# Merging a head's softmax parts on 32 partitions in layer 2's cross attention

## The chip, the core and the metric

The kernel runs on one core of a Trainium2 chip. A core has five engines with a queue each: TensorE (PE in the profile, its weight loads PEld), VectorE (DVE), ScalarE (ACT), GpSimd (POOL) and SyncE (SP, which issues most DMAs). They work side by side and wait for each other by semaphores. The metric is the device time of one execution in microseconds (us), the median of several runs.

## What is computed

Four layers of cross attention and feed-forward on an input x of 4 x 256 x 256, all in float32. The change lies in the cross attention of layer 2:

```python
q = rope(rms_norm((x @ wq).reshape(B, L, 16, 128)))     # B = 4, L = 256
k_full = [rms_norm(ctx @ wk_ctx), rope(rms_norm(x @ wk))]   # 1601 + 256 keys, 4 heads of keys
v_full = [ctx @ wv_ctx, x @ wv]
scores = jnp.einsum('bhlm,...', q, k_full) * scale + mask   # own keys causal
probs = jax.nn.softmax(scores, axis=-1)
out = jnp.einsum('bhlm,bmhd->blhd', probs, v_full)
return out.reshape(B, L, 16 * 128) @ wo
```

That is shortened: rope is applied to q and to the own keys, not to the keys of the context, and each key head serves four query heads. A softmax over one query's keys needs their maximum and the sum of their exponentials.

## The kernel before

The stage `l2_xattn` works through 16 units: batch 0 to 3 by key head 0 to 3, and in a unit through four query heads h, 64 heads in all. A unit's keys `kT` and values `va` have 15 tiles of 128 keys.

A head's 256 queries are cut into 8 blocks of 32, two blocks to each of four steps c. In `scores` (lines 1451 to 1475) the products of one block with all keys are spread over the partitions: partition 32a + j holds query j of the block against the keys 32a to 32a+31 of each tile. So each query lies on four partitions, one in each group of 32. Every partition finds the negated maximum of its own part (`nm`, line 1467, VectorE) after the mask is added (line 1464), and ScalarE computes the exponentials `p` with it and sums them up (`sm`, line 1471). There are two pairs of score banks (`ps_s`, `bufs=2`): the product for step c waits until the exponentials of step c-2 have been read from theirs.

The four parts of a query then have to be merged. `merge` (1477 to 1501) does it for a whole head: TensorE transposes `nm` and `sm` (each 128 partitions x 8 blocks) to 8 partitions x 128 in PSUM (`tm`, lines 1482 and 1483); VectorE takes the least negated maximum of the four parts (`lo`, 1487) and the differences (1489), ScalarE the exponentials of these (`em`, 1490); VectorE multiplies them with the sums (1492), adds the four parts (1494), takes the reciprocal (1495) and multiplies (1496). That gives each part's share, still as 8 x 128. TensorE transposes it back (1498), and VectorE copies it to `rm`, 128 x 8 (1500).

GpSimd then scales the eight `p` blocks with these shares (`scale`, line 1507), VectorE transposes them in squares of 32 x 32 (`turn`, 1513), and TensorE multiplies with the values into `o` (`values`, lines 1517 to 1526; 30 instructions), which ScalarE copies to `at`. Every four heads `project` multiplies with `wo` and adds to x.

The heads are overlapped by generators: while the scores of head h are issued, `softmax_steps` of head h-1 and `value_steps` of head h-2 are advanced, and between them `prep` prepares queries, own keys and loads for the next unit. A step of a generator ends at `yield`. In the main loop, `softmax_steps` is advanced once after the scores of c = 0 and 1 (the first part of `merge`, up to its `yield`), a second time at the end of this half, after values, preparation and projection (the rest of `merge` and the scalings), and a third time after the scores of c = 2 and 3 (the turns). The source order sets priorities; each engine's final order is made by a list scheduler when the program is built, except where `keep_in_program_order` pins an instruction. So in the profile `lo` stands between a mask and its maximum.

[...] 4 for scores, 2 for preparation (`ps`), 1 for `tm` (`ps_m`) and 1 for `o` (`ps_o`).

Of the kernel before, what the change touches and what calls it, by code (L numbers as in the profile page):

```python
# [11 lines left out]
F32 = mybir.dt.float32  # L12
# [5 lines left out]
AF = mybir.ActivationFunctionType  # L18
ALU = mybir.AluOpType
AX = mybir.AxisListType  # L20
PSUM = bass.MemoryType.PSUM
DRAM = bass.MemoryType.DRAM

P = 128
# [34 lines left out]
class Kernel:  # L59
# [1185 lines left out]
    def l2_xattn(self):  # L1245
# [8 lines left out]
        nc, tc, i = self.nc, self.tc, self.i  # L1254
        NK, CT = NK2, CT2
        OWN = [(13, 32, P), (14, 160, 96)]
        with ExitStack() as es:
# [1 line left out]
            two = es.enter_context(tc.tile_pool(name="a2", bufs=2, reuse_waits="tile"))  # L1259
            ps_s = es.enter_context(tc.tile_pool(name="a2s", bufs=2, space=PSUM))  # L1260
            ps = es.enter_context(tc.tile_pool(name="a2p", bufs=2, space=PSUM))
            ps_m = es.enter_context(tc.tile_pool(name="a2m", bufs=1, space=PSUM))
            ps_o = es.enter_context(tc.tile_pool(name="a2o", bufs=1, space=PSUM))
            self.take = lambda: ps_s.tile([P, 2, 512], F32, name="fill2", tag="s2")[:, 0, :]

            mask = one.tile([P, 8, 3, 32], F32, name="mask2")
# [41 lines left out]
            def load(g, early):  # L1308
                w = {}
                for n, shape in (("wq", [P, 2, 512]), ("wkc", [P, 2, 256]), ("wks", [P, 2, 256])):  # L1310
                    if n == "wkc" and early:
                        continue
                    w[n] = one.tile(shape, F32, name=n)
                    nc.sync.dma_start(w[n], i["l2_" + n][g])
                return w
# [131 lines left out]
            def tiles_of(c):  # L1447

                return 14 if c < 2 else 15

            def scores(kT, qT, h, c, nm, sm):

                nt = tiles_of(c)
                s = ps_s.tile([P, 2, 512], F32, name="s2")
                for n in range(2):
                    q0 = (2 * c + n) * 32
                    for a in range(4):
                        self.mm(
                            s[32 * a : 32 * a + 32, n, : nt * 32].rearrange("p (t i) -> p t i", i=32),
                            qT[:, h, q0 : q0 + 32], kT[:, :nt, 32 * a : 32 * a + 32], True, True,  # L1460
                        )
                w = (nt - CT) * 32
                sv = s[:, :, CT * 32 : nt * 32]
                nc.vector.tensor_tensor(  # L1464
                    sv, sv, mask[:, 2 * c : 2 * c + 2, : nt - CT, :].rearrange("p n t i -> p n (t i)"), ALU.add
                )
                nc.vector.tensor_reduce(nm[:, 2 * c : 2 * c + 2], s[:, :, : nt * 32], AX.X, ALU.max, negate=True)  # L1467
                p = main.tile([P, 2, NK * 32], F32, name="p2", bufs=8)
                for n in range(2):
                    e = 2 * c + n  # L1470
                    nc.scalar.activation(  # L1471
                        p[:, n, : nt * 32], s[:, n, : nt * 32], AF.Exp, bias=nm[:, e : e + 1],
                        accum_out=sm[:, e : e + 1],
                    )
                return p

            def merge(nm, sm):


                t = ps_m.tile([P, 512], F32, name="tm2")  # L1480
                ct, st = t[:8, 0:P], t[:8, P : 2 * P]
                tc.keep_in_program_order(nc.tensor.transpose(ct, nm, self.ident))
                tc.keep_in_program_order(nc.tensor.transpose(st, sm, self.ident))
                by = lambda ap: ap.rearrange("n (a j) -> n j a", a=4)
                wide = lambda ap: ap[:, :, None].to_broadcast([8, 32, 4])
                lo = self.small.tile([8, 32], F32, name="lo2")
                nc.vector.tensor_reduce(lo, by(ct), AX.X, ALU.min)
                e = self.small.tile([8, P], F32, name="em2", bufs=2)
                nc.vector.tensor_tensor(by(e), wide(lo), by(ct), ALU.subtract)
                nc.scalar.activation(e, e, AF.Exp)  # L1490
                w = self.small.tile([8, P], F32, name="wm2", bufs=2)
                nc.vector.tensor_tensor(w, e, st, ALU.mult)
                tot = self.small.tile([8, 32], F32, name="tot2")
                nc.vector.tensor_reduce(tot, by(w), AX.X, ALU.add)
                nc.vector.reciprocal(tot, tot)
                nc.vector.tensor_tensor(by(e), by(e), wide(tot), ALU.mult)
                yield
                nc.tensor.transpose(t[:, 256:264], e, self.ident[:8, :8])
                r = self.small.tile([P, 8], F32, name="rm2")
                nc.vector.tensor_copy(r, t[:, 256:264])  # L1500
                return r

            def scale(p, r, c):
                nt = tiles_of(c)
                for n in range(2):
                    e = 2 * c + n
                    nc.gpsimd.tensor_scalar(  # L1507
                        p[:, n, : nt * 32], p[:, n, : nt * 32], r[:, e : e + 1], 1.0, ALU.mult, ALU.mult
                    )

            def turn(p, pT, c):
                nt = tiles_of(c)
                nc.vector.transpose(  # L1513
                    pT[:, 2 * c : 2 * c + 2, :nt, :].rearrange("p n t i -> p n (t i)"), p[:, :, : nt * 32]
                )
# [23 lines left out]
            def softmax_steps(hd):  # L1539


                shares = merge(hd["nm"], hd["sm"])
                next(shares)
                yield
                r = yield from shares
                hd["pT"] = main.tile([P, 8, NK, 32], F32, name="pT2")
                for c in range(4):
                    scale(hd["p"][c], r, c)
                yield
                for c in range(4):  # L1550
                    turn(hd["p"][c], hd["pT"], c)
                yield
# [9 lines left out]
            w = load(0, True)  # L1562
            wo = load_out(0)
# [13 lines left out]
            for n, (b, g) in enumerate(units):  # L1577
                kT, va, qT = ready
                last = hd
                ready, pieces = [], None  # L1580
                wo_now = wo
                at = main.tile([P, 4, S], F32, name="at2", bufs=2)
                for h in range(4):
                    hd = {"nm": self.small.tile([P, 8], F32, name="nm2"), "sm": self.small.tile([P, 8], F32, name="sm2"),
                          "p": [], "va": va, "at": at, "h": h, "b": b, "wo": wo_now}
                    for c in (0, 2):
                        step = 2 * h + c // 2
                        for cc in (c, c + 1):
                            hd["p"].append(scores(kT, qT, h, cc, hd["nm"], hd["sm"]))
                        if soft is not None:  # L1590
                            next(soft[0])
                        if pieces is not None and not early:
                            for _ in range(BETWEEN[step]):
                                next(pieces, None)
                        if vals is not None:
                            next(vals)
                        if step == 0 and n + 1 < len(units):
                            b1, g1 = units[n + 1]
                            early = n + 1 < EARLY
                            if not early and (b1 != b or ctx is None):  # L1600
                                ctx = self.load_ctxT(one, b1, 1)
                            w = load(g1, early)
                            pieces = prep(n + 1, w, ctx, ready)
                            if g1 == 0:
                                next(pieces)
                        if step == 4 and n + 1 < len(units):
                            wo = load_out(g1)
                        if pieces is not None:
                            for _ in range((WHEN_EARLY if early else WHEN)[step]):
                                next(pieces, None)  # L1610
                        if step == 5 and last is not None:
                            project(last)
                        if soft is not None and c == 0:
                            next(soft[0])
                    vals = value_steps(soft[1]) if soft is not None else None
                    soft = (softmax_steps(hd), hd)
                if pieces is not None:
                    for _ in pieces:
                        pass
# [595 lines left out]
```

## Time and profile before

| what | us |
|---|---|
| median of 3 runs | 2638.49 (2635.17 to 2639.96) |
| profiled execution, its own time | 2638.45 |
| its span, first to last instruction | 2636.7 |
| layer 2's attention loop, by the trace | about 695 to 1805 |
| TensorE busy over the span | 2491.9 (95%) |
| VectorE | 1480.0 (56%) |
| ScalarE | 1310.9 (50%) |
| GpSimd | 750.8 (28%) |

A few of the groups that the change touches, with the mean duration of one instruction in the stage (64 of each, one for a head): the two transposes into `tm` 273 ns each by the record, the one back 221; `lo` 275, the differences 355, the exponential 293, the product 275, the sum over parts 377, the reciprocal 338, the shares 364, the copy to `rm` 161. Around them, for one head: 8 exponentials of 645 ns on ScalarE, 8 scalings of 657 on GpSimd, 4 turns of 1127 and 4 maxima of 1104 on VectorE.

A row of the profile names the source line, the engine, the operation, the tile written and the tiles read, shapes, count, busy time and mean, and behind the bar the time the engine stood idle before these instructions with what ended most of it. Matmuls overlap in the array, so the durations of their records are longer than their part of the stream; the part is the distance from one start to the next.

### The profile page before, as it was taken

Reading aid. Unit: us, or ns where it says so; the run is one execution under the profiler, and the core shown is the slowest. Engines: PE = TensorE matmul, PEld = TensorE weight load, DVE = VectorE, ACT = ScalarE, POOL = GpSimd, SP = SyncE. Lnnn points to the kernel's source line nnn. Section 1 sums busy time; section 2 is a strip of 40 time slices with the busy share of each in tenths; the row PEclk is TensorE's granted clock in tenths of the full one; section 3 lists DMA queues with packets and bytes.
Section 4 is the critical chain, followed back from the end, with each engine's and each line's share of the span. In section 5 each row is a group of like instructions: output and inputs, shape, how many; then the busy total and the mean of one; then the engine's idle time right before and its main releaser. Section 6 shows DMA issues by size and latency. Waiting matters only on the chain. (4 is left out here: it accounts for less than half of the span.)

```text
span 2636.7 us, 47077 instructions
## 1 busy us (share of the span) xinstructions
PE 2491.9 (95%) x17816; PEld 1517.6 (58%) x17816; DVE 1480.0 (56%) x3039; ACT 1310.9 (50%) x2957; POOL 750.8 (28%) x1030
## 2 busy tenths in 40 slices
PE   7989988898799999999999999998998999999997
PEld 4668967676455555555555555655564544545553
DVE  6344637644587777777777777673334414333323
ACT  2334545433644445444544454442326766757775
POOL 1015646123334343334443434431102001011000
PEclk8989999999999999999999999998999999999998
DMA  5154787615511111111111110004211100000000
GB/s 201 60 199 128 186 174 216 205 56 174 162 38 46 39 37 46 46 38 47 46 46 46 46 46 21 9 1 159 87 66 63 34 2 27 4 3 2 6 6 5
DMA packets 94655, 186.25 MB, mean 71 GB/s; under 512 B 15052, under 2 KB 62864, under 8 KB 93232
## 3 DMA queue, kind: packets, MB, share of 16 engines
q1 hardware_dynamic: 78118, 141.36, 15.8%
q0 software_dynamic: 10416, 28.46, 5.0%
q10 hardware_dynamic: 5898, 13.41, 1.5%
q8 instruction: 145, 2.38, 0.4%
q14 instruction: 78, 0.64, 0.1%
HBM read 136.77 MB, written 46.42 MB: 69 GB/s over the span
## 5 line engine op out<-in xcount | busy, mean ns | idle before, releaser
L1471 ACT ACTIVATE p<-s,nm 128x448 f32<-128x448 f32 (+1 forms) x512 | 326.9, 645 | 423.9 <-DVE nm L1467 259.1
L1932 ACT ACTIVATE e<-s 128x1024 f32<-128x1024 f32 (+1 forms) x448 | 404.2, 960 | 160.8 <-PE s L75 156.1
L75 PE MATMUL s<-kT,qT 128*32 128x448 f32 (+1 forms) x4096 | 470.2, 556 | 10.0 <-ACT p L1471 5.0
L75 PE MATMUL o<-pT,va 128*128 128x256 f32 (+2 forms) x1920 | 432.5, 377 | 6.1 <-DVE pT L1513 6.1
L1507 POOL TENSOR_SCALAR p<-p,rm 128x448 f32<-128x448 f32 (+1 forms) x512 | 323.7, 657 | 369.6 <-DVE rm L1500 339.4
L75 PEld LDWEIGHTS o<-pT,va 128*128 128x128 f32 (+1 forms) x1920 | 345.4, 191 | 93.6 <-issue 51.5
L1513 DVE STREAM_TRANSPOSE pT<-p 128x896 f32<-128x896 f32 (+1 forms) x256 | 283.8, 1127 | 37.1 <-POOL p L1507 33.4
L1467 DVE TENSOR_REDUCE nm<-s 128x2 f32<-128x896 f32 (+1 forms) x256 | 282.6, 1104 | 3.4
L75 PE MATMUL s<-qb,kT 32*128 32x256 f32 (+1 forms) x3328 | 267.7, 405 | 11.0 <-ACT e L1932 11.0
L75 PEld LDWEIGHTS s<-kT,qT 128*32 128x32 f32 x4096 | 123.6, 109 | 265.0 <-issue 222.5
L75 PE MATMUL o<-e,va 128*32 128x256 f32 (+1 forms) x3328 | 236.6, 392 | 1.2 <-DVE os L2029 1.2
L75 PEld LDWEIGHTS s<-qb,kT 32*128 32x128 f32 (+1 forms) x3328 | 163.1, 181 | 105.5 <-issue 75.8
L75 PE MATMUL fill<-wkc_early,ctxT 128*128 128x256 f32 x780 | 189.6, 401 | 11.8 <-ACT kT_early L1227 9.6
L75 PEld LDWEIGHTS fill<-wkc_early,ctxT 128*128 128x128 f32 x780 | 152.1, 199 | 43.1 <-ACT kT_early L1227 15.0
L75 PEld LDWEIGHTS o<-e,va 128*32 128x32 f32 (+1 forms) x3328 | 90.8, 110 | 115.5 <-issue 75.5
L1959 POOL TENSOR_TENSOR x<-x,t 128x32 f32<-128x32 f32 x64 | 14.7, 252 | 439.7 <-DVE t L1954 439.7
L1464 DVE TENSOR_TENSOR s<-s,mask 128x128 f32<-128x128 f32 (+1 forms) x256 | 83.1, 325 | 67.1 <-PE s L75 62.3
L410 POOL DMA_INDIRECT f0xr<-f0xd,f0src x95 | 92.3, 972 | 51.3 <-PE f0tph L467 43.2
L1359 POOL TENSOR_TENSOR qo<-qo,qt 128x512 f32<-128x512 f32 x32 | 40.7, 1273 | 230.6 <-DVE rm L1500 139.4
L1471 ACT ACTIVATION_READ_ACCUMULATOR p<-s,nm 128x1 f32 x512 | 101.7, 199 | 0.0
L1200 ACT COPY kr_early<-fill 128x256 f32<-128x256 f32 (+1 forms) x105 | 37.3, 355 | 97.9 <-PE fill L75 97.7
L75 PE MATMUL f2gu<-f2wgu,f2xsT 128*128 x176 | 84.3, 603 | 0.6 <-ACT f2xsT L72 0.3
(510 smaller groups left out, 3503.7 us busy)
## 6 DMA issues: line engine op xcount, KB each, us to landing
ctxT<-in_ctxT SPq DMA_DIRECT2D x10, 1664.0 KB
f0yd<-f0ys SPq DMA_DIRECT2D x95, 128.0 KB
vd<-va_early SPq DMA_DIRECT2D x90, 128.0 KB
kd<-kT_early SPq DMA_DIRECT2D x45, 256.0 KB
kT<-kd SPq DMA_DIRECT2D x15, 768.0 KB
va<-vd SPq DMA_DIRECT2D x15, 768.0 KB
wq<-in_l_wq SPq DMA_DIRECT2D x16, 512.0 KB
wo<-in_l_wo SPq DMA_DIRECT2D x16, 512.0 KB
```

What stands on the lines that cost most here:

```text
L75: self.nc.tensor.matmul(out, lhsT, rhs, start=start, stop=stop, **kw)
L410: nc.gpsimd.indirect_dma_start(out=t, out_offset=None, in_=xd[:, :], in_offset=bass.IndirectOffsetOnAxis(ap=src[:, n : n + 1], axis=0),)
L1200: nc.scalar.copy(kr[:rows, m : m + n, :], tp[:rows, :n, :HD2])
L1359: nc.gpsimd.tensor_tensor(o1, o1, t2, ALU.add)
L1464: nc.vector.tensor_tensor(sv, sv, mask[:, 2 * c : 2 * c + 2, : nt - CT, :].rearrange("p n t i -> p n (t i)"), ALU.add)
L1467: nc.vector.tensor_reduce(nm[:, 2 * c : 2 * c + 2], s[:, :, : nt * 32], AX.X, ALU.max, negate=True)
L1471: nc.scalar.activation(p[:, n, : nt * 32], s[:, n, : nt * 32], AF.Exp, bias=nm[:, e : e + 1], accum_out=sm[:, e : e + 1],)
L1507: nc.gpsimd.tensor_scalar(p[:, n, : nt * 32], p[:, n, : nt * 32], r[:, e : e + 1], 1.0, ALU.mult, ALU.mult)
L1513: nc.vector.transpose(pT[:, 2 * c : 2 * c + 2, :nt, :].rearrange("p n t i -> p n (t i)"), p[:, :, : nt * 32])
L1932: nc.scalar.activation(e[:kr, :, :n, :], s[t][:kr, :, :n, :], AF.Exp, scale=1.0 / math.sqrt(HD3))
L1959: nc.gpsimd.tensor_tensor(xt, xt, t[:, q], ALU.add)
```

## The change

The two small tiles `nm` and `sm` become one tile `ms` of 128 x 2 x 8. `merge` no longer uses TensorE: VectorE copies the four groups of 32 partitions side by side onto partitions 0 to 31 (`c`, 32 x 4 x 2 x 8, four copies of 32 x 16), so that a query's four parts lie on one partition. Minimum, difference, exponential, product, sum and reciprocal then run on 32 partitions with 32 elements or 8, and the shares are written back with four multiplications of 32 x 8, one to each group of partitions of `rm`. The `yield` moves: it stood in front of the transpose back, and stands now behind the exponential, so that product, sum, reciprocal and shares belong to the second step. The PSUM bank of `tm` goes to `o`, which has two banks now.

```diff
-            ps_m = es.enter_context(tc.tile_pool(name="a2m", bufs=1, space=PSUM))
-            ps_o = es.enter_context(tc.tile_pool(name="a2o", bufs=1, space=PSUM))
+            ps_o = es.enter_context(tc.tile_pool(name="a2o", bufs=2, space=PSUM))
...
-                nc.vector.tensor_reduce(nm[:, 2 * c : 2 * c + 2], s[:, :, : nt * 32], AX.X, ALU.max, negate=True)
+                nc.vector.tensor_reduce(ms[:, 0, 2 * c : 2 * c + 2], s[:, :, : nt * 32], AX.X, ALU.max, negate=True)
...
-                        p[:, n, : nt * 32], s[:, n, : nt * 32], AF.Exp, bias=nm[:, e : e + 1],
-                        accum_out=sm[:, e : e + 1],
+                        p[:, n, : nt * 32], s[:, n, : nt * 32], AF.Exp, bias=ms[:, 0, e : e + 1],
+                        accum_out=ms[:, 1, e : e + 1],
...
-                t = ps_m.tile([P, 512], F32, name="tm2")
-                ct, st = t[:8, 0:P], t[:8, P : 2 * P]
-                tc.keep_in_program_order(nc.tensor.transpose(ct, nm, self.ident))
-                tc.keep_in_program_order(nc.tensor.transpose(st, sm, self.ident))
-                by = lambda ap: ap.rearrange("n (a j) -> n j a", a=4)
-                wide = lambda ap: ap[:, :, None].to_broadcast([8, 32, 4])
-                lo = self.small.tile([8, 32], F32, name="lo2")
-                nc.vector.tensor_reduce(lo, by(ct), AX.X, ALU.min)
-                e = self.small.tile([8, P], F32, name="em2", bufs=2)
-                nc.vector.tensor_tensor(by(e), wide(lo), by(ct), ALU.subtract)
+                c = self.small.tile([32, 4, 2, 8], F32, name="ms2")
+                for a in range(4):
+                    nc.vector.tensor_copy(c[:, a], ms[32 * a : 32 * a + 32])
+                by = lambda ap: ap.rearrange("j a n -> j n a")
+                wide = lambda ap: ap[:, None, :].to_broadcast([32, 4, 8])
+                lo = self.small.tile([32, 8], F32, name="lo2")
+                nc.vector.tensor_reduce(lo, by(c[:, :, 0]), AX.X, ALU.min)
+                e = self.small.tile([32, 4, 8], F32, name="em2")
+                nc.vector.tensor_tensor(e, wide(lo), c[:, :, 0], ALU.subtract)
                 nc.scalar.activation(e, e, AF.Exp)
-                w = self.small.tile([8, P], F32, name="wm2", bufs=2)
-                nc.vector.tensor_tensor(w, e, st, ALU.mult)
-                tot = self.small.tile([8, 32], F32, name="tot2")
+                yield
+                w = self.small.tile([32, 4, 8], F32, name="wm2")
+                nc.vector.tensor_tensor(w, e, c[:, :, 1], ALU.mult)
+                tot = self.small.tile([32, 8], F32, name="tot2")
                 nc.vector.tensor_reduce(tot, by(w), AX.X, ALU.add)
                 nc.vector.reciprocal(tot, tot)
-                nc.vector.tensor_tensor(by(e), by(e), wide(tot), ALU.mult)
-                yield
-                nc.tensor.transpose(t[:, 256:264], e, self.ident[:8, :8])
                 r = self.small.tile([P, 8], F32, name="rm2")
-                nc.vector.tensor_copy(r, t[:, 256:264])
+                for a in range(4):
+                    nc.vector.tensor_tensor(r[32 * a : 32 * a + 32], e[:, a], tot, ALU.mult)
                 return r
```

The callers pass `ms` in place of the two tiles.

More of the change, by code (lines that the diff above doesn't have):

```diff
@@ L1449, in tiles_of, with scores @@
                 return 14 if c < 2 else 15
-            def scores(kT, qT, h, c, nm, sm):
+            def scores(kT, qT, h, c, ms):
                 nt = tiles_of(c)
@@ L1471, in scores @@
                     nc.scalar.activation(
-                        p[:, n, : nt * 32], s[:, n, : nt * 32], AF.Exp, bias=nm[:, e : e + 1],
-                        accum_out=sm[:, e : e + 1],
-                    )
-                return p
-            def merge(nm, sm):
-                t = ps_m.tile([P, 512], F32, name="tm2")
-                ct, st = t[:8, 0:P], t[:8, P : 2 * P]
-                tc.keep_in_program_order(nc.tensor.transpose(ct, nm, self.ident))
-                tc.keep_in_program_order(nc.tensor.transpose(st, sm, self.ident))
-                by = lambda ap: ap.rearrange("n (a j) -> n j a", a=4)
-                wide = lambda ap: ap[:, :, None].to_broadcast([8, 32, 4])
-                lo = self.small.tile([8, 32], F32, name="lo2")
-                nc.vector.tensor_reduce(lo, by(ct), AX.X, ALU.min)
-                e = self.small.tile([8, P], F32, name="em2", bufs=2)
-                nc.vector.tensor_tensor(by(e), wide(lo), by(ct), ALU.subtract)
+                        p[:, n, : nt * 32], s[:, n, : nt * 32], AF.Exp, bias=ms[:, 0, e : e + 1],
@@ new lines, in scores, with merge @@
+                        accum_out=ms[:, 1, e : e + 1],
+                    )
+                return p
+            def merge(ms):
+                c = self.small.tile([32, 4, 2, 8], F32, name="ms2")
[7 more added lines that the diff above has]
+                nc.vector.tensor_tensor(e, wide(lo), c[:, :, 0], ALU.subtract)
@@ L1539, in softmax_steps @@
             def softmax_steps(hd):
-                shares = merge(hd["nm"], hd["sm"])
+                shares = merge(hd["ms"])
                 next(shares)
@@ L1583, in l2_xattn @@
                 for h in range(4):
-                    hd = {"nm": self.small.tile([P, 8], F32, name="nm2"), "sm": self.small.tile([P, 8], F32, name="sm2"),
-                          "p": [], "va": va, "at": at, "h": h, "b": b, "wo": wo_now}
+                    hd = {"ms": self.small.tile([P, 2, 8], F32, name="nmsm2"), "p": [], "va": va, "at": at, "h": h, "b": b,
+                          "wo": wo_now}
                     for c in (0, 2):
@@ L1588, in l2_xattn @@
                         for cc in (c, c + 1):
-                            hd["p"].append(scores(kT, qT, h, cc, hd["nm"], hd["sm"]))
+                            hd["p"].append(scores(kT, qT, h, cc, hd["ms"]))
                         if soft is not None:
```

## The prediction

> **What bounds the kernel now.** I read the slices and the busy shares first, then the stage that the change touches (from 695 to 1805 us, 64 heads), then the single starts on TensorE, then who waits there. By stretches (start, middle, end of the stage; sum and mean are left out):
>
> ```profile
> core 0: us, PE busy (x) PEld busy (x) DVE busy (x) ACT busy (x) POOL busy (x), PEclk, DMA share, GB/s
> 695.00:740.00 45.00, 37.39 (x288) 16.00 (x281) 36.40 (x61) 24.95 (x69) 17.02 (x24) 1.00 0.15 50
> 740.00:1620.00 880.00, 873.90 (x5608) 483.28 (x5607) 673.57 (x1140) 422.22 (x1192) 354.06 (x514) 1.00 0.14 44
> 1620.00:1805.00 185.00, 177.69 (x1107) 109.25 (x1105) 125.67 (x206) 71.62 (x204) 65.15 (x106) 0.98 0.02 7
> ```
>
> TensorE is busy 99% of the 880 us in the middle at full clock, VectorE 77%, ScalarE 48%, GpSimd 40%. A busy share of TensorE can mislead, since its records overlap, so the second look is at starts. The timeline of PE alone in three short windows (start, duration, what):
>
> ```profile
> 1301.82 0.56 PE L75 MATMUL s<-kT,qT 128*32 128x448 f32 x4
> 1302.31 0.27 PE L1482 MATMUL tm<-ident,nm 128*8 128x128 f32 x1
> 1302.42 0.27 PE L1483 MATMUL tm<-ident,sm 128*8 128x128 f32 x1
> 1302.53 0.38 PE L75 MATMUL o<-pT,va 128*128 128x256 f32 x1
> ...
> 1307.05 0.57 PE L75 MATMUL s<-kT,qT 128*32 128x480 f32 x1
> 1307.54 0.22 PE L1498 MATMUL tm<-ident,em 8*128 8x8 f32 x1
> 1307.70 0.61 PE L75 MATMUL s<-kT,qT 128*32 128x480 f32 x4
> ...
> 1309.34 0.97 PE L75 MATMUL s<-kT,qT 128*32 128x480 f32 x5
> 1310.24 0.48 PE L75 MATMUL o<-pT,va 128*128 128x256 f32 x1
> ```
>
> Nothing waits in these lines: a group of four score products takes 0.37 us (448 columns) or 0.40 (480), an o product of 256 columns 0.21, and each next instruction starts as soon as the columns before it are through. Over the middle of the stage the single starts leave hardly more than these fixed steps. Waits of TensorE in the whole stage, from the list of waits:
>
> ```profile
> PEld s L75 <- ACT p L1471: 20.1, 41, 2.5
> PE o L75 <- DVE pT L1513: 6.1, 5, 2.4
> PE s L75 <- ACT p L1471: 5.0, 4, 2.2
> PE tm L1498 <- DVE em L1496: 1.9, 4, 0.6
> ```
>
> So the middle is bound by what TensorE is given. The start (37 of 45 us) and the end (178 of 185) hang in part on chains: the last merge is followed by scaling, turns and 9.5 us of o products.
>
> [...] kt (L1405, two SBUF inputs), median 559 ns, took 1329 when it started behind a running GpSimd addition. [...]
>
> **What goes, per head.** On TensorE: the two first transposes, 0.109 + 0.109 us of stream (the step from s into the next kind, 0.49 at 448 columns, stays: s to o direct has it too, 0.50 at 480). The third: from the last s group before it to the s after it 0.65 us (1307.05 to 1307.70), where two s groups follow each other in 0.40: 0.25. Between o products, as in 15 heads, it is 0.31 + 0.15 in place of 0.21: 0.25 as well. Sum 0.47 us, times 64 = 30 us. On VectorE seven operations go: lo 275 ns, difference 355, product 275, tot 377, reciprocal 338, share 364, copy of r 161: 2.15 us. ScalarE's exp of 8x128 (293 ns) becomes one of 32x32; a 128x32 copy there takes 192 (L1440), so 0.1 less, hidden on an engine at 48%.
>
> **What comes, per head.** Thirteen VectorE operations on 32 partitions. No row has them[...]. What goes with it is a wait: VectorE stood still for the exp of the merge,
>
> ```profile
> DVE wm L1492 <- ACT em L1490: 100.1, 64, 2.5
> ```
>
> 1.56 us a head. The product now stands behind the yield, so other work can be put before it; the price is that the product, tot, reciprocal and shares are issued after the query preparation of that step (three operations of 0.68), up to 2 us later in a head with a preparation. Queued behind them are GpSimd's eight scalings, then VectorE's four turns and TensorE's o.
>
> **Slack against that.** From the end of a head's last turn to its first o product the trace has at least 2.05 us in every head of the middle (at 1302 us: turns end at 1315.8, o starts at 1318.0). From the end of an exp that frees a score bank to the score product that takes it I find 0.8 us at the least, two places in a unit of four heads under 1.3, the rest 1.5 to 5.5. The chain to r also gets shorter by what it need no longer wait for: the transposes stand behind the next head's scores on TensorE (sums done at 1298.8, first transpose 1302.3), the third behind an s group, and r is ready at 7 to 13 us after the sums. So the turns should rather come earlier. An earlier turn (1.1 us) can stand before a mask or maximum once and then eat the 0.8: I charge 4 us in all.
>
> **Ends.** Heads 0, 1 and 63 don't give their 0.47 (their o waits for turns): -1.4. In place of it the chain there: at 724 us o waits 2 us for turns, and the chain to r can shorten by about 3; in the last head sums to r take 4.6 us (1780.3 to 1784.9)[...]. Together +3. The second o bank costs and gives nothing: no o product waits for the copy of at in the list of waits. No DMA, no instruction of SP's queue and no order of loads is moved; the stages after this one shift.
>
> **Sum.** 30 + 3 - 4 = 29 us off the profiled run's 2638.45 us (span 2636.7), which is the median of the runs shown, 2638.49, to 0.1: 2609.
>
> **Rivals.**
> *Given back to the score banks.* TensorE runs 0.47 us a head ahead, the exps don't, and the slack of 0.8 is nearly gone; with turns falling between masks and maxima half the gain returns: 2638 - 14 = 2624. For: VectorE at 77%. Against: the freed 1.56 us.
> [...] If GpSimd is scaling when they come, each waits up to one scaling of 0.66 us; the copies and the difference alone then hold the queue 3.3 us, and the masks and maxima behind them are late where the slack is 0.8 to 1.2, in half the heads: about 2.3 us x 32 - 29 = +45, 2683. It decides from a mean TensorE stall over 0.47 us a head. For: one head in four has the scalings before it running past its sums. Against: in the other three GpSimd waits for r just then (339 us of waits for rm).
> *More than the transposes.* If the earlier r also takes away the leftover waits for p and the start's 8 us: 2638 - 42 = 2596.
> *No effect* would need the transposes to lie in gaps of TensorE, which the starts above exclude.
>
> **Numbers.** Forecast 0.66 (its own range 2602 to 2618), half given back 0.13, slower 0.13, more 0.08. The range 2597 to 2630 holds the first two and most of the last. What a measurement can tell from no change is about 0.2%, 5 us: faster 0.82, same 0.05, slower 0.13.
>
> **What would show it.** No tm rows; s to o steps of 0.47 to 0.50 us; the middle of the stage shorter by 0.4 to 0.5 us a head; VectorE without the 100 us for em; sums to r under 6 us in most heads. Wrong would be: waits of s for p above 60 us, durations of the new copies or shares well over 0.2 us with GpSimd running, or o waiting for turns in the middle.

## The result, and the profile after

The changed kernel takes 2629.38 us, median of 13 runs (2621.64 to 2632.4), against 2636.85 (2631.51 to 2645.4) for the kernel before beside it: a ratio of 0.997, interval 0.9961 to 0.9979. That is 7.5 us faster where 29 were forecast. The profiled execution took 2629.74 us, its span is 2628.0.

The stage in the same three stretches (a row gives from and to, length, then busy time and count for each engine):

```profile
core 0: us, PE busy (x) PEld busy (x) DVE busy (x) ACT busy (x) POOL busy (x), PEclk, DMA share, GB/s
695.00:740.00 45.00, 35.94 (x257) 13.90 (x255) 33.56 (x67) 24.24 (x67) 16.99 (x24) 0.96 0.16 56
740.00:1620.00 880.00, 831.64 (x5478) 468.31 (x5479) 692.88 (x1457) 418.74 (x1188) 356.71 (x519) 1.00 0.14 44
1620.00:1805.00 185.00, 173.57 (x1102) 109.42 (x1101) 131.56 (x282) 75.04 (x215) 61.87 (x101) 0.98 0.05 17
```

In the middle TensorE is now busy 94.5% of the time where it was busy 99.3%: it was given less, and it stands still for the difference. What it waits for is in the list of waits of the changed kernel over the stage (engine, tile and line, the work waited for, us in total, times, longest):

```profile
PEld s L75 <- ACT p L1470: 112.0, 114, 3.9
...
DVE ms L1482 <- ACT p L1470: 83.5, 58, 3.2
...
PE s L75 <- ACT p L1470: 60.7, 48, 3.1
...
DVE wm L1492 <- ACT em L1489: 17.0, 39, 2.1
...
PE o L75 <- DVE pT L1511: 2.8, 2, 2.4
```

The score products wait for the exponentials that free their banks: 112.0 + 60.7 us on TensorE's two queues, where it was 20.1 + 5.0. The two queues wait side by side (at 1088.37 us both go on, one after 1.52 us, the other after 2.37), so this is not the loss itself. The wait for `em` shrank from 100.1 to 17.0 us as forecast, and a new one came, 83.5 us of the first copy waiting for the exponential that writes the last sums.

To get the loss, I added up TensorE's single starts over eleven repeating units (44 heads), from the first o product of the third unit to that of the fourteenth. "Columns" is the time of everything issued at the pace of full streams (a group of 480 columns 0.40 us, one of 256 columns 0.21), "small gaps" is what single steps take above it, up to 0.35 us each, and "stalls" is each longer gap.

| 11 units, us | before | after |
|---|---|---|
| whole | 753.1 | 751.6 |
| columns | 696.2 | 659.7 |
| small gaps | 50.5 | 42.0 |
| stalls | 6.3 | 49.8 |

So TensorE was given 36.5 + 8.5 = 45.0 us less, more than twice the forecast 0.47 x 44 = 20.7, and the stalls grew by 43.5 us; all 38 stalls of the changed kernel stand before score products. The middle hardly changed (1.5 us). Of the 7.8 us by which the stage became shorter, from its first score product to the end of the last projection, 6.0 lie behind the fourteenth unit's first o product, 3.7 of them in the last unit and its tail, and 0.3 in the start.

Where one stall comes from is seen in the timeline (start, duration, engine, line, what) of a unit's last head, steps 0 and 1. VectorE in the kernel before:

```profile
1077.92 0.30 DVE L1464 TENSOR_TENSOR s<-s,mask 128x128 f32<-128x128 f32 x1
1078.26 1.09 DVE L1467 TENSOR_REDUCE nm<-s 128x2 f32<-128x896 f32 x1
1079.42 0.30 DVE L1464 TENSOR_TENSOR s<-s,mask 128x128 f32<-128x128 f32 x1
1079.64 0.28 DVE L1487 TENSOR_REDUCE lo<-tm 8x32 f32<-8x128 f32 x1
1079.84 1.07 DVE L1467 TENSOR_REDUCE nm<-s 128x2 f32<-128x896 f32 x1
```

The same head in the changed kernel, with ScalarE and TensorE:

```profile
1082.00 0.28 DVE L1463 TENSOR_TENSOR s<-s,mask 128x128 f32<-128x128 f32 x1
1082.32 1.09 DVE L1466 TENSOR_REDUCE nmsm<-s 128x2 f32<-128x896 f32 x1
1083.53 1.11 DVE L1511 STREAM_TRANSPOSE pT<-p 128x896 f32<-128x896 f32 x1
1084.57 0.27 DVE L1463 TENSOR_TENSOR s<-s,mask 128x128 f32<-128x128 f32 x1
1084.77 1.11 DVE L1511 STREAM_TRANSPOSE pT<-p 128x896 f32<-128x896 f32 x1
1085.81 1.05 DVE L1466 TENSOR_REDUCE nmsm<-s 128x2 f32<-128x896 f32 x1
...
1086.97 0.63 ACT L1470 ACTIVATE p<-s,nmsm 128x448 f32<-128x448 f32 x1 [2.11 <-PE s L75]
1087.60 0.63 ACT L1470 ACTIVATE p<-s,nmsm 128x448 f32<-128x448 f32 x1
...
1088.37 1.82 PE L75 MATMUL s<-kT,qT 128*32 128x480 f32 x16 [1.52 <-ACT p L1470]
```

Two turns of the head before, 1.11 us each, stand in front of the second mask and the second maximum. The exponentials of step 1 wait for that maximum and begin at 1086.97; the products of step 3 wait 1.52 us for the bank that these read. In the 44 heads, the turns between the mask of step 0 and the maximum of step 1 number 0 in the kernel before and 44 in the changed one: two in the first and the last head of every unit, none in the two between. From the start of the last product of step 1 to its first exponential it is 2.69 us before and 5.34 after, on the average. The turns come this early because r is ready earlier: from the last sums to r it takes 5.05 us in place of 11.39.

The stalls follow these turns, but not all of them do. Of the 49.8 us, 40.4 lie in the 22 heads with two turns. The other 9.4 lie in 11 heads without a turn, where a table load of ScalarE (`ACT_TABLE_LOAD` in the profile) stands between the maximum of step 0 and its exponential. The row of these loads has 19 of 1283 ns in the stage:

```profile
L1470 ACT ACT_TABLE_LOAD x19 | 24.4, 1283 | 13.1 <-DVE nmsm L1466 9.3 <-DVE rm L1498 2.5 <-DVE tot L1494 1.2
```

The 11 heads with neither have no stall. In the kernel before, 14 of the 44 heads have such a load and none of them stalls, so the load alone does not make a stall. That it counts now because there is less slack is argued, not shown.

### The profile page after: what moved, and what is told of

It is laid out like the page before. It is cut to its first block, busy times and chain, and to the rows that moved or that the text cites. A ratio compares the mean times of both kernels' runs of the same rounds, so it can differ in the third digit from the quotient of the medians.

```text
span 2628.0 us, 47046 instructions
## 1 busy us (share of the span) xinstructions
PE 2431.8 (93%) x17608; PEld 1494.9 (57%) x17624; DVE 1496.5 (57%) x3423; ACT 1307.8 (50%) x2957; POOL 749.1 (29%) x1030
## 5 line engine op out<-in xcount | busy, mean ns | idle before, releaser
L1470 ACT ACTIVATE p<-s,nmsm 128x448 f32<-128x448 f32 (+1 forms) x512 | 326.6, 644 | 478.2 <-DVE nmsm L1466 401.2
L75 PE MATMUL s<-kT,qT 128*32 128x448 f32 (+1 forms) x4096 | 434.7, 560 | 63.3 <-ACT p L1470 60.7
L75 PE MATMUL o<-pT,va 128*128 128x256 f32 (+2 forms) x1920 | 439.6, 379 | 2.8 <-DVE pT L1511 2.8
L1505 POOL TENSOR_SCALAR p<-p,rm 128x448 f32<-128x448 f32 (+1 forms) x512 | 323.3, 659 | 359.9 <-DVE rm L1498 350.8
L1511 DVE STREAM_TRANSPOSE pT<-p 128x896 f32<-128x896 f32 (+1 forms) x256 | 289.3, 1135 | 82.2 <-POOL p L1505 77.0
L75 PEld LDWEIGHTS s<-kT,qT 128*32 128x32 f32 x4096 | 117.2, 110 | 321.8 <-issue 197.9
L1466 DVE TENSOR_REDUCE nmsm<-s 128x2 f32<-128x896 f32 (+1 forms) x256 | 282.8, 1109 | 3.1
L75 PE MATMUL fill<-wkc_early,ctxT 128*128 128x256 f32 x780 | 187.0, 397 | 12.2 <-ACT kT_early L1227 10.0
L1470 ACT ACTIVATION_READ_ACCUMULATOR p<-s,nmsm 128x1 f32 x512 | 101.4, 198 | 0.0
L1482 DVE COPY ms<-nmsm 32x16 f32<-32x16 f32 x256 | 43.7, 171 | 86.1 <-ACT p L1470 83.5
```

The costliest lines, as they stand in the source:

```text
L75: self.nc.tensor.matmul(out, lhsT, rhs, start=start, stop=stop, **kw)
L1466: nc.vector.tensor_reduce(ms[:, 0, 2 * c : 2 * c + 2], s[:, :, : nt * 32], AX.X, ALU.max, negate=True)
L1470: nc.scalar.activation(p[:, n, : nt * 32], s[:, n, : nt * 32], AF.Exp, bias=ms[:, 0, e : e + 1], accum_out=ms[:, 1, e : e + 1],)
L1482: nc.vector.tensor_copy(c[:, a], ms[32 * a : 32 * a + 32])
L1505: nc.gpsimd.tensor_scalar(p[:, n, : nt * 32], p[:, n, : nt * 32], r[:, e : e + 1], 1.0, ALU.mult, ALU.mult)
L1511: nc.vector.transpose(pT[:, 2 * c : 2 * c + 2, :nt, :].rearrange("p n t i -> p n (t i)"), p[:, :, : nt * 32])
```

## The experiments

Three theories. A: the earlier turns in VectorE's queue make the maxima and so the exponentials late. B: the copies of `ms`, which wait for the last sums at the head of VectorE's queue, hold up the next head's masks and maxima. C: the copies and the shares are slowed when instructions of GpSimd run beside them. Beside these, what the transposes cost in the kernel before was open (theory D in what was expected of e4), since TensorE's load had fallen by twice what I had counted.

**e1: the turns are queued behind the maximum of step 1 (theory A).** Only VectorE's order changes. `self.mx2[c]` keeps the maximum's instruction of each step of the newest head; in `softmax_steps`:

```diff
-                for c in range(4):
-                    turn(hd["p"][c], hd["pT"], c)
+                with tc.issue_after(self.mx2[1]):
+                    for c in range(4):
+                        turn(hd["p"][c], hd["pT"], c)
```

> The changed kernel with one more constraint: a head's four turns are queued on VectorE behind the maximum of step c = 1 of the next head, so no turn stands between these masks and maxima. Theory A (the earlier turns delay the next head's maxima, its exponentials free the score banks late and TensorE waits): the waits of s for p fall from 173 us (61 on the products, 112 on the weight loads) to under 60, and the time from 2629 to 2575 to 2600. Rival B (VectorE stands at the copies, waiting for the last sums, 84 us in all, and the masks behind them are late): the copies are untouched, so 2622 to 2632. Rival C[...]: no change either, 2622 to 2632.

Measured: 2583.92 us (2581.66 to 2587.28), ratio to before 0.980 (0.9778 to 0.9822). The same head in e1, VectorE alone:

```profile
1065.99 0.28 DVE L1463 TENSOR_TENSOR s<-s,mask 128x128 f32<-128x128 f32 x1
1066.31 1.09 DVE L1466 TENSOR_REDUCE nmsm<-s 128x2 f32<-128x896 f32 x1
1067.32 0.29 DVE L1463 TENSOR_TENSOR s<-s,mask 128x128 f32<-128x128 f32 x1
1067.64 1.09 DVE L1466 TENSOR_REDUCE nmsm<-s 128x2 f32<-128x896 f32 x1
1068.65 2.10 DVE L1511 STREAM_TRANSPOSE pT<-p 128x896 f32<-128x896 f32 x2
```

In none of the 44 heads does a turn stand between the first mask and the second maximum now. From the start of the last product of step 1 to its exponential it takes 3.47 us on the average. And e1's list of waits:

```profile
DVE ms L1482 <- ACT p L1470: 82.3, 58, 3.2
...
PEld s L75 <- ACT p L1470: 48.8, 87, 3.9
```

TensorE's stalls fall from 49.8 to 15.0 us over the 44 heads, at the same 659.7 us of columns, and the stretch takes 713.2 us. A holds for most of the loss. The copies' wait is still there in full, 82.3 us, so B is not the main cause. Where that wait lies says the same: in the 44 heads of the changed kernel, VectorE stands idle for the copies less than 0.1 us in all between the last product of step 0 and the maximum of step 1. Of e1's 15.0 us of stalls, 7.1 wait for exponentials, in five heads, each with a table load before the exponential; the other 7.9 stand at the start of eight units, where the first score product waits for the copies into `kT`.

**e2: the copies are queued behind that maximum (theory B).**

```diff
-                next(shares)
+                with tc.issue_after(self.mx2[1]):
+                    next(shares)
```

> The changed kernel with the first part of the merge (copies, minimum, difference) queued on VectorE behind the maximum of step c = 1 of the next head, where the kernel before had it in effect. The wait of the copies for the last sums goes, and r and the turns come later. Theory A: the turns fall again between the masks and maxima of steps 2 and 3, as before the change, where there was slack; waits of s for p under 90 us, time 2580 to 2610. Rival B (the wait at the copies is the cost): the wait of 84 us falls to under 10 and the time to 2575 to 2600, below the run with the turns held back. Rival C: 2622 to 2632.

Measured: 2583.58 us (2581.99 to 2584.8), ratio 0.9801 (0.9779 to 0.9822): as fast as e1, to 0.3 us. Its waits:

```profile
PEld s L75 <- ACT p L1470: 40.8, 60, 3.4
...
PEld o L75 <- DVE pT L1511: 19.0, 16, 1.9
```

The copies' wait is gone from the list and the stalls of score products with it. That alone would fit B too, but the edit also makes r later (sums to r 8.59 us) and with it the turns: none stands between the two maxima any more. As e1 gets the same time with the copies' wait left in, the turns explain most of both. No stall of e2 waits for an exponential, where e1 has 7.1 us of them; whether the copies' wait has an indirect part in these is not shown. e2 pays elsewhere: 10.2 us of its 12.2 us of stalls are o products that now wait for turns.

**e3: one o bank instead of two.** The second half of the change, undone alone.

```diff
-            ps_o = es.enter_context(tc.tile_pool(name="a2o", bufs=2, space=PSUM))
+            ps_o = es.enter_context(tc.tile_pool(name="a2o", bufs=1, space=PSUM))
```

> The changed kernel with one bank for o, as before the change. All theories: no o product waited for the copy of at, so 2624 to 2634, no difference from 2629 that can be told. If the second bank carried the gain (o products issued ahead): 2634 or more.

Measured: 2610.08 us (2605.7 to 2612.55), ratio 0.9901 (0.9877 to 0.9926): by the two ratios the changed kernel is 18 us faster with one bank than with two. The waits of its score products for p are 89.7 + 42.1 us on the two queues where they were 112.0 + 60.7, and the stalls are 30.9 us instead of 49.8. The maxima don't explain it: 50 turns stand between those of steps 0 and 1, not fewer than the 44. Nor does TensorE's other work between the products of steps 1 and 2: 3.80 us a head with two banks, 3.86 with one. What does differ is how soon VectorE gets to the first maximum: from the end of the last product of step 0 to the end of its maximum it takes 3.88 us a head with two banks and 3.32 with one. The turns take 0.68 and 0.75 us of that; the difference lies in the rest of the merge and other small operations on VectorE that stand there. How a bank of `o` brings that order about, and whether it is all of the 18 us, the runs do not isolate.

**e4: the kernel before, with its third transpose moved out of the group of products.** Here nothing of the change is in. The transpose back keeps its place of the source, and the source puts it between the products of steps 2 and 3:

```diff
-                nc.tensor.transpose(t[:, 256:264], e, self.ident[:8, :8])
+                tc.keep_in_program_order(nc.tensor.transpose(t[:, 256:264], e, self.ident[:8, :8]))
...
                             hd["p"].append(scores(kT, qT, h, cc, hd["nm"], hd["sm"]))
+                            if soft is not None and cc == 2:
+                                next(soft[0])
...
-                        if soft is not None and c == 0:
-                            next(soft[0])
```

> The kernel before, with the transpose of the shares back issued between the score products of steps 2 and 3 of the next head, not after the fifth of the eight products of step 2. Theory D (TensorE bounds the kernel before, and a transpose that splits a group of four column products makes the lone product take a whole pass, twice 0.40 us in three heads of four, so the three transposes cost 1.05 us a head and not 0.47): some 48 heads x 0.8 = 38 us less, less what a later r costs: 2597 to 2612 from 2637. Rival E (the lone products cost nothing, as the records only show them apart): 2632 to 2640.

Measured: 2606.04 us (2604.86 to 2608.28), ratio 0.9887 (0.9865 to 0.991), with all three transposes still there. Why is read from TensorE's timeline at the place that the prediction showed. The kernel before, with its weight loads below:

```profile
1305.81 1.80 PE L75 MATMUL s<-kT,qT 128*32 128x480 f32 x10
1307.54 0.22 PE L1498 MATMUL tm<-ident,em 8*128 8x8 f32 x1
1307.70 2.62 PE L75 MATMUL s<-kT,qT 128*32 128x480 f32 x22
...
1306.24 0.11 PEld L75 LDWEIGHTS s<-kT,qT 128*32 128x32 f32 x1 [0.27 <-issue]
1306.64 0.11 PEld L75 LDWEIGHTS s<-kT,qT 128*32 128x32 f32 x1 [0.29 <-issue]
```

And e4, between the products of steps 2 and 3 of another head:

```profile
1303.12 1.82 PE L75 MATMUL s<-kT,qT 128*32 128x480 f32 x16
1304.86 0.23 PE L1498 MATMUL tm<-ident,em 8*128 8x8 f32 x1
1305.02 1.82 PE L75 MATMUL s<-kT,qT 128*32 128x480 f32 x16
```

A step has 8 products, four side by side in a group (one on each quarter of the array's columns: 128*32 in the rows, where an o product has 128*128), and each product leaves two records, so a step has 16, in four passes of a group. In the kernel before, the transpose stands behind the fifth product: 10 records take 1.73 us (1305.81 to 1307.54), in e4 16 records take 1.74. The fifth product's two passes cost 0.40 us each although only a quarter of the array is used, and the three others pay the same once more behind the transpose: the next 22 records take 2.54 us (1307.70 to 1310.24), six passes. A pass of four products and a pass of one both take 0.40 us here, so a group cut in two costs twice. In 33 of the 44 heads the transpose had cut a group, 66 passes of 0.40 us, 26.4 us; e4's columns are 669.8 us, just these 26.4 below before, and its 44 heads take 726.1.

The last three runs were on another chip, where the kernel before takes 2683.77 us. What comes ahead of the stage takes some 45 us longer there (e7 beside the changed kernel), while the stage is as long as on the first, 1100.1 us in e7 and 1101.2 in the changed kernel; so ratios and the stage's own times are compared.

**e5: e1 with one o bank.** Both edits together.

> The turns queued behind the next head's second maximum and o back to one bank. If what one bank gave (2610 against 2629) was only that another order of TensorE put fewer turns between masks and maxima, it has nothing more to give once the turns are held back: 2580 to 2588, as with two banks. If the second bank costs by itself, by letting o products and preparations be ordered so that score products come late: 2560 to 2575.

Ratio 0.9817 (0.9787 to 0.9846), the 44 heads 713.9 us, e1's 713.2. Once the turns are held back, the number of o banks no longer matters. The part of this expectation that takes e3's gain for one of fewer turns between the maxima is not borne out, as the count under e3 says.

**e6: e2 with one o bank.**

> The copies queued behind the next head's second maximum and o back to one bank. As in the run with the turns: 2578 to 2588 if the bank acts only through the turns, 2560 to 2575 if it costs by itself. The waits of o for turns (14 us with two banks) may grow, since r is late here.

Ratio 0.9853 (0.9817 to 0.9889), the 44 heads 720.5 us where e2 has 713.9. With the later r one bank is slower in these profiled executions: score products stall 7.1 us where they had 2.0, o products 8.6 where they had 10.2, and small gaps grow by 3.0 us. The intervals of the two ratios just meet, so the whole times alone would not settle it.

**e7: the `yield` put late.** It moves from behind the exponential to behind the reciprocal, so that only the shares are in the second step:

```diff
                 nc.scalar.activation(e, e, AF.Exp)
-                yield
                 w = self.small.tile([32, 4, 8], F32, name="wm2")
...
                 nc.vector.reciprocal(tot, tot)
+                yield
```

> The changed kernel with the yield behind the reciprocal, so that product, sum and reciprocal belong to the first step as before the change and only the four shares to the second. The list scheduler takes what is ready, so r comes hardly earlier or later and turns still fall between masks and maxima: 2620 to 2640. If the place of the yield (merge work behind the query preparation) is what costs: 2600 or less.

Ratio 0.9972 (0.9963 to 0.998), the changed kernel's own; 50.1 us of stalls, 44 turns between the maxima, sums to r 5.05 us. Moving the `yield` there changes nothing that can be measured in this kernel.

| 44 heads, us | whole | columns | small gaps | stalls |
|---|---|---|---|---|
| e1 turns behind the maximum | 713.2 | 659.7 | 38.5 | 15.0 |
| e2 copies behind it | 713.9 | 659.7 | 42.0 | 12.2 |
| e3 one o bank | 733.7 | 659.7 | 43.1 | 30.9 |
| e4 before, group whole | 726.1 | 669.8 | 51.7 | 4.6 |
| e7 yield late | 751.9 | 659.7 | 42.1 | 50.1 |

Theory C had no run of its own; the durations answer it. The rows of the shares and copies in the changed kernel (forms, count, busy us, mean ns, idle time before):

```profile
L1498 DVE TENSOR_TENSOR rm<-em,tot 32x8 f32<-32x8 f32 x256 | 52.9, 207 | 4.6
L1482 DVE COPY ms<-nmsm 32x16 f32<-32x16 f32 x256 | 43.7, 171 | 86.1 <-ACT p L1470 83.5
```

Their medians are 157 and 163 ns, so the means are raised by 50 and 8 ns; of 512 copies and shares 19 took over 0.5 us. C is there but small: e1 has 28 of them and is among the fastest.

## Why the prediction was wrong

The direction was right and so was most of the mechanism. The size was wrong by two terms that missed in opposite senses.

- **"Sum 0.47 us, times 64 = 30 us."** Too small by more than half. TensorE was relieved of 45.0 us in 44 heads, 1.02 a head, and of 48.5 with the turns held back (e1: 36.5 of columns and 12.0 of small gaps), 1.10 a head. The third transpose was priced at 0.25 by the delay around it. The group that it cuts was left out: 66 x 0.40 us over 44 heads is 0.60 a head, and 0.47 + 0.60 = 1.07. The sign of it stood in the lines that the prediction quotes: a score record "x1" at 1307.05 directly in front of `tm`, where the others come in fours.
- **"An earlier turn (1.1 us) can stand before a mask or maximum once and then eat the 0.8: I charge 4 us in all."** This is the step that failed. It names the mechanism and gives it a tenth of its size: 43.5 us of new stalls over 44 heads. Two things were wrong in it. It let a turn come between once, and there are 44 in 44 heads, two in every second one. And it set the slack of 0.8 us against the old load; with TensorE relieved of 1.0 us a head that slack is used up before the first turn comes, which would let each delay of an exponential count in full (that part is argued, the runs show only the sum). e1 takes that delay away and gets 34.8 us of it back. ScalarE's table load of 1.28 us before some of the exponentials is not in the prediction at all; 9.4 us of the stalls lie in heads with a load and no turn.
- **The range and the rivals.** "Given back to the score banks" is what happened. It was given 0.13 and half the gain; in the middle of the stage 43.5 of 45.0 us were given back. The rival at 2683 us (the new operations waiting for GpSimd's scalings) and "more than the transposes" did not decide. e1 and e2 gain more than the 42 us of the second, but not mainly in its way: their 44 heads save 26.4 us of passes that the cut groups had cost, and stalls are 15.0 and 12.2 us where the kernel before has 6.3. The 2596 of that rival lies outside the range from 2597, which is said to hold most of it.
- **What comes on VectorE.** What the prediction charged for the thirteen operations was the author's estimate; no trace of the kernel before showed it. Measured, they take 4 x 171 + 194 + 178 + 193 + 192 + 186 + 4 x 207 = 2455 ns a head, 0.3 us more than the 2.15 us that go. Four copies in a row, each from another group of 32 partitions:

```profile
1078.82 0.69 DVE L1482 COPY ms<-nmsm 32x16 f32<-32x16 f32 x4 [1.46 <-ACT p L1470]
```

  Each begins 13 or 14 ns after the end of the one before (all 187 such pairs), the shares after 13 to 32 ns, while operations of the query preparation that follow each other on all partitions begin 70 to 83 ns before that end. So copies do not overlap with each other here, nor do shares, while those operations do; the gaps of 13 to 32 ns add little to durations of 171 and 207 ns.
- **The wait for `em`** went as said, and the exponential takes 224 ns. That "up to 2 us" of delay by the moved `yield` mattered neither way (e7).
- **Ends, +3 - 1.4.** By the marks of the accounting, 6.3 us were gained outside the eleven units (0.3 at the start, 6.0 at the end). That is nearly all of the measured gain. These parts include 20 heads that lose their transposes as well, so the chain's own share is not separated.
- **"The second o bank costs and gives nothing."** Wrong in the changed kernel: it costs 18 us (e3). Right once the turns are held back (e5); with the copies held back instead, the second bank saves 6.6 us in the 44 heads (e6).
- **What would show it.** No `tm` row, sums to r at 5.05 us on the average of the 44 heads and under 6 in 35 of all 64 (before, it was 8.0 to 13.9 in all but the last head, where the prediction reads 7 to 13), o waiting for turns only 2.8 us: these came out as said. The step from s to o is 0.49 us at 448 columns and 0.52 at 480, the second a little over the 0.50 named. The middle is 0.03 us a head shorter instead of 0.4 to 0.5, and the waits of s for p passed the 60 us named as a sign against it. The shares' mean is 207 ns with GpSimd's part in it, barely over the 0.2 named.

Open is how the second o bank lengthens the stalls, and what of the 15.0 us of stalls left in e1 could still go: the 7.1 behind table loads and the 7.9 behind the copies into `kT`.

The version to keep is e1 or e2: the change with one edge added to VectorE's order, 52 us or 2.0% below the kernel before, against 0.3% without it. The relief of TensorE alone is not enough: e1 has the same instructions as the changed kernel. And most of e1's gain needs no change of the merge: of the 39.9 us that its 44 heads are shorter than before, 27.0 come in e4 as well, which keeps all three transposes.

## What to carry to other kernels

The small transpose among products that share the array in groups cost more here than the 0.25 us that it was priced at: in the 33 heads where it cut a group, two more passes of 0.40 us each. Look at whether a small matmul cuts a group. When a chain is made shorter, ask what becomes ready earlier and in front of what it will be queued; work without urgency that is ready early can stand ahead of the operation on which the bound engine waits (here two turns of 1.11 us ahead of a maximum). Slack measured beside the old load may not be the slack of the new one: take what the bound engine gains off it first.

## What the runs showed of the hardware

A share of 32x8 takes 157 ns in the median and up to 1153. The timeline of the changed kernel at one of the long ones:

```profile
908.59 1.31 DVE L1498 TENSOR_TENSOR rm<-em,tot 32x8 f32<-32x8 f32 x2
908.61 1.27 POOL L1358 TENSOR_TENSOR qo<-qo,qt 128x512 f32<-128x512 f32 x1 [12.52 <-PE s L75]
```

The second of the two shares starts at 908.75 and ends at 909.90, with the addition on GpSimd at 909.88. All 20 copies and shares that start while a GpSimd instruction runs end like this, within 0.03 us after one of GpSimd, and 19 of them (16 shares, 3 copies) take over 0.5 us. What holds them is not shown. I had not expected the wait to be so rare: 17 of the 256 shares start while an instruction of GpSimd runs, and its scalings wait 350.8 us in all for the shares. The other surprise is the lone product that e4 does away with: a quarter of the array for 0.40 us, as long as a whole group.
